# Reading a transposed operand in runs of eight: the column-major half of a four-way scan's input projection

## The chip, the cores and the metric

The kernel runs on one core of a Trainium2 chip. The core has five engines that run side by side, each with a queue of its own that it works through strictly in order: TensorE (PE, matrix products, with weight loads listed apart as PEld), VectorE (DVE), ScalarE (ACT), GpSimd (POOL) and SyncE (SP, which here only starts DMA transfers). Engines wait for one another through semaphores. Operands lie in the on-chip memory (SBUF, 128 partitions). TensorE writes its products into PSUM, and ACT or DVE take them out from there; this is called an eviction. The metric is the device time of one execution in microseconds.

## The reference, cut to what matters

The network takes images x of shape (8, 64, 64, 96): eight images of 64 by 64 points with 96 channels. The part that the change touches is the input of a selective scan in four directions:

```
xz = einsum('bhwc,ec->bhwe', group_norm(x), in_proj_w)      # 96 -> 2 * 192
xin, z = split(xz, 2)
xc = silu(depthwise_conv3x3(xin) + conv_b)                  # b, 192, h, w
x_hw = xc.reshape(b, 192, 4096)                             # row-major
x_wh = transpose(xc, (0, 1, 3, 2)).reshape(b, 192, 4096)    # column-major
xs = stack([x_hw, x_wh, flip(x_hw), flip(x_wh)])            # four directions
x_dbl = einsum('bkdl,kcd->bkcl', xs, x_proj_weight)         # 192 -> 6 + 16 + 16 per direction
dts, Bs, Cs = split(x_dbl, [6, 22])
```

Behind that come the step sizes delta = softplus(dt_proj(dts)), the scan h = h * exp(delta * A) + delta * u * B with y = sum(h * C) over 16 states, the sum of the four directions, a normalization, a gate and an output projection, and then an attention block and a small quantized feed-forward block. Everything is in float32 where the change is made. The flipped directions use the same u and only other weights, so the kernel makes two projections per image: o = 0 over u in row-major order and o = 1 over u in column-major order, each for two directions at once.

## The kernel before, in words

The kernel has three passes, one behind the other. `pass1` (line 233) makes everything that the scans need: group norm, input projection, convolution with SiLU, x_proj, and the splitting of its results into bfloat16 parts. `pass2` (line 513) does the scans, `pass3` (line 819) the rest. The change lies in pass 1 alone.

Channels lie on the partitions. Images are taken in pairs. The 192 channels of a pair fill three chunks of 128 partitions: chunk 0 and chunk 1 are the first 128 channels of the two images, chunk 2 holds the last 64 of both. The order is 0, 2, 1 (`ORDER`, line 248). One chunk of u is a tile of 128 x 4096 (h, w row-major); four of these may be open at a time (`UB`, line 238).

- `projection` (line 348) transposes 512 points of x on TensorE (`pt`), normalizes them on DVE (`xn`), multiplies them by the weights (`pa`) and lets ACT evict them into the padded image `xpad` and the gate `z`. `statistics` (line 305) does the same transposes ahead of that (`xs`, `pt`), and DVE takes the group statistics `st`; `group_norm` finishes them through two tiny products (`pm`, `pv`).
- `convolution` (line 397) makes nine DVE instructions of 128 x 4096 for one chunk, and then on ACT the SiLU: four instructions that read a quarter of the columns of u and write it, turned to column-major, into `ut` (two buffers, each stored to `u_d[b][1]` by SP), then two instructions that put SiLU onto u in place, half by half, and a store of u to `u_d[b][0]`. The bookkeeping marks u as finished (`done["u", ...]`) with the last of these.
- `x_projection` (line 445) takes 512 points of one image and one order: two products that add up in one PSUM bank `px` (three banks), an eviction to `xd` (three buffers) by ACT, or by DVE for every second group of the last pair, and a store to `xd_d`. For o = 1 the product reads u with a step of one image row, 64 float32 values, from each element to the next. Each float32 product appears in the trace as two records.
- `split` (line 469) loads rows of `xd_d` back (`bq`), rounds them on ACT (`bs`), subtracts on POOL (for the last image on DVE) and stores the parts.

The instructions of each engine are issued in an order that is fixed when the program is built. `weave` (line 140) is a small planner: each unit (one call of the functions above) announces its next step with an engine and an assumed cost in microseconds (`yield "act", 2.1`), and the planner always issues the step that could begin first by its own clock. So a changed cost in a `yield` changes the order of instructions on every engine in pass 1. The class `InOrder` (line 81) issues each of them, which is why nearly all rows of the profile carry line 89; its rows are told apart by tile names. Passes 2 and 3 have plans of their own and issue the same instructions in the same order in both kernels.

Of the kernel before, what the change touches and what calls it, by code (L numbers as in the profile page):

```python
# [33 lines left out]
F32 = mybir.dt.float32  # L34
# [3 lines left out]
AF = mybir.ActivationFunctionType  # L38
# [4 lines left out]
P = 128  # L43
NB, HH, WW, C = 8, 64, 64, 96
L = HH * WW
DI, N, R, K = 192, 16, 6, 4
NXD = R + 2 * N
# [11 lines left out]
RPG = GRP // WW  # L59
# [6 lines left out]
def chunk_rows(pair, c):  # L66

    b0 = 2 * pair
    if c < 2:
        return [(slice(0, P), b0 + c, slice(0, P))]  # L70
    return [(slice(64 * j, 64 * j + 64), b0 + j, slice(P, DI)) for j in range(2)]
# [161 lines left out]
def pass1(ctx, tc, g, consts, ident, mhalf, engines, u_d, z_d, xd_d, b_d, dt_d):  # L233
    nc = tc.nc
    pe, dve, act, pool = engines
    sp = InOrder(tc, nc.sync)
# [3 lines left out]
    two = ctx.enter_context(tc.tile_pool(name="p1two", bufs=2))  # L240
# [19 lines left out]
    conv_b = wp.tile([P, 2, 1], F32, name="conv_b")  # L260
# [26 lines left out]
    pts, mms, pxs = Slots(2), Slots(3), Slots(3)  # L287
    counts = {}

    def one_more(key, of, end):  # L290
        counts[key] = counts.get(key, 0) + 1
        if counts[key] == of:
            done[key] = end
# [103 lines left out]
    def convolution(pair, c):  # L397

        ty = c // 2
        src = xpad[c + pair % 2 if c == 2 else c]  # L400
        for b in [2 * pair, 2 * pair + 1] if c == 2 else [2 * pair + c]:
            yield "proj", b
        before = {0: (pair - 1, 1), 2: (pair, 0), 1: (pair, 2)}[c]
        at = 3 * pair + ORDER.index(c) - UB
        if at >= 0:
            old, c_old = at // 3, ORDER[at % 3]
            for b in {0: (2 * old,), 1: (2 * old + 1,), 2: (2 * old, 2 * old + 1)}[c_old]:
                yield "xproj", b
            yield "stored", old, c_old
        if before[0] >= 0:  # L410
            yield "conv", *before
        u = None
        for tap in range(9):
            end = yield "dve", 2.6 if tap == 0 else 4.4, 0.0
            if tap == 0:
                u = us_p.tile([P, L], F32, name="u")
                us[pair, c] = u
                uv = u.rearrange("p (h w) -> p h w", w=WW)
            win = src[:, tap // 3 : tap // 3 + HH, tap % 3 : tap % 3 + WW]
            if tap == 0:  # L420
                dve.tensor_scalar(uv, win, conv_w[:, ty, tap : tap + 1], None, ALU.mult)
            else:
                dve.scalar_tensor_tensor(uv, win, conv_w[:, ty, tap : tap + 1], uv, ALU.mult, ALU.add)
        done["conv", pair, c] = end
        if before[0] >= 0:
            yield "stored", *before
        parts = chunk_rows(pair, c)
        for w in (slice(i, i + WW // 4) for i in range(0, WW, WW // 4)):
            yield "act", 2.1
            ut = two.tile([P, L // 4], F32, name="ut")  # L430
            act.activation(ut.rearrange("p (w h) -> p h w", h=HH), uv[:, :, w], AF.Silu, bias=conv_b[:, ty, :])
            yield "sp", 0.5
            for part, b, ch in parts:
                sp.dma_start(u_d[b][1][ch, w.start * HH : w.stop * HH], ut[part, :])
        for h in range(2):
            cols = slice(h * (L // 2), (h + 1) * (L // 2))
            end = yield "act", 2.0
            act.activation(u[:, cols], u[:, cols], AF.Silu, bias=conv_b[:, ty, :])
        done["u", pair, c] = end
        end = yield "sp", 0.5  # L440
        for part, b, ch in parts:
            sp.dma_start(u_d[b][0][ch, :], u[part, :])
        done["stored", pair, c] = end

    def x_projection(b, o, q):
        pair, j = b // 2, b % 2
        yield "u", pair, j
        yield "u", pair, 2
        px = None
        for ty, u in ((0, us[pair, j]), (1 + j, us[pair, 2])):  # L450
            end = yield ("pe", 0.9, 0.4) if px else ("pe", 0.9, 0.4, pxs)
            if px is None:
                px, slot = ps_px.tile([P, GRP], F32, name="px", tag="px"), pxs.taken
            if o == 0:
                src = u[:, q * GRP : (q + 1) * GRP]
            else:
                src = u.rearrange("p (h w) -> p w h", w=WW)[:, q * RPG : (q + 1) * RPG, :]
            pe.matmul(px, w_xp[:, ty, o, :], src, start=ty == 0, stop=ty > 0)
        one_more(("xproj", b), 2 * NG, end)
        by_dve = pair == NB // 2 - 1 and q % 2 == 1  # L460
        end = yield ("dve" if by_dve else "act"), 0.6
        xd = three.tile([2 * NXD, GRP], F32, name="xd")
        (dve.tensor_copy if by_dve else act.copy)(xd, px[0 : 2 * NXD, :])
        pxs.release(slot, end)
        end = yield "sp", 0.9, 3.0
        sp.dma_start(xd_d[b][o][:, q * GRP : (q + 1) * GRP], xd)
        one_more(("xd", b, o), NG, end)
# [26 lines left out]
    for pair in range(NB // 2):  # L494
        batches = (2 * pair, 2 * pair + 1)
        for b in batches:
            units += [("stats", statistics(b, q)) for q in range(NG)]
            units.append(("norm", group_norm(b)))
            units += [("proj", projection(b, q)) for q in range(NG)]
        for c in ORDER:  # L500
            units.append(("conv", convolution(pair, c)))
        for b in batches:
            for o in range(2):
                units += [("xproj", x_projection(b, o, q)) for q in range(NG)]
                units += [("split", split(b, o, 0, 2 * N, 4, at, b_d[b][o])) for at in (0, GRP)]
                units.append(("split", split(b, o, DT0, 2 * R, 8, 0, dt_d[b][o])))
# [595 lines left out]
```

## Time and profile before

| What | Value |
|---|---|
| Time, median of 8 runs | 10575.13 us (10571.86 to 10589.52) |
| The profiled execution's own time | 10577.66 us |
| Its span, first to last instruction | 10575.9 us |
| Mean granted TensorE clock | 0.899 of full |
| Pass 1, until the first loads of pass 2 can start | about 830 us of the span |
| Busy over the span | DVE 91%, ACT 88%, POOL 88%, PE 73% |

The busy shares of the whole span are those of pass 2, which takes most of it. What the change can move is decided in the first 830 us, and for these the views are asked for single stretches. A "records" count of a tile named px counts two for each product. "A <- B" in a list of waits means that an instruction writing A stood idle until B was done. The chain of waits is followed backwards from the last instruction of a window, so it shows in each stretch what ended last there.

### The profile page before, as it was taken

Reading aid. Unit: us, or ns where it says so; the run is one execution under the profiler, and the core shown is the slowest. Engines: PE = TensorE matmul, PEld = TensorE weight load, DVE = VectorE, ACT = ScalarE, POOL = GpSimd, SP = SyncE. Lnnn points to the kernel's source line nnn. Section 1 sums busy time; section 2 is a strip of 40 time slices with the busy share of each in tenths; the row PEclk is TensorE's granted clock in tenths of the full one; section 3 lists DMA queues with packets and bytes.
Section 4 is the critical chain, followed back from the end, with each engine's and each line's share of the span. In section 5 each row is a group of like instructions: output and inputs, shape, how many; then the busy total and the mean of one; then the engine's idle time right before and its main releaser. Section 6 shows DMA issues by size and latency. Waiting matters only on the chain.

```text
span 10575.9 us, 151369 instructions
## 1 busy us (share of the span) xinstructions
PE 7706.9 (73%) x51232; PEld 6204.6 (59%) x51232; DVE 9635.6 (91%) x6994; ACT 9299.9 (88%) x21355; POOL 9258.9 (88%) x3259
## 2 busy tenths in 40 slices
PE   6876777777677777777677777776777777776887
PEld 3325666566556666666566666665566666555775
DVE  7767999999999999999999999999999999997776
ACT  4648999999999999999999999999999999996665
POOL 2547999999999999999999999999999999997886
PEclk8988999998999999988999999889999999987776
DMA  5756666679986666698966666889766667997442
GB/s 153 218 184 196 209 212 218 209 216 200 197 216 213 212 215 209 213 206 195 211 216 209 217 212 216 206 199 205 216 211 210 219 208 216 201 199 178 127 125 64
DMA packets 928009, 2103.22 MB, mean 199 GB/s; under 512 B 274391, under 2 KB 422648, under 8 KB 925700
## 3 DMA queue, kind: packets, MB, share of 16 engines
q1 hardware_dynamic: 919812, 2092.79, 70.7%
q8 instruction: 410, 6.72, 0.3%
q14 instruction: 363, 2.97, 0.1%
q10 hardware_dynamic: 7424, 0.74, 0.1%
HBM read 1917.59 MB, written 175.66 MB: 198 GB/s over the span
## 4 chain that ended last, share of the span: by engine, by line
ACT 28%; DVE 21%; PE 18%; issue 17%; POOL 13%; DMA 3%; SPq 1%; DVEq 0%; ACTq 0%; POOLq 0%
DVE h L89 15%; ACT x L89 13%; ACT da L89 10%; POOL c L89 9%; PE wide L89 6%; PE acc L89 6%; DVE wide L89 3%; PE px L89 2%; PE mm L89 2%; ACT L89 1%; DMA xdt<-dt_d 1%; PE pa L89 1%; POOL xg L89 1%; DVE u L89 1%; ACT delta L89 1%
## 5 line engine op out<-in xcount | busy, mean ns | idle before, releaser
L89 POOL TENSOR_TENSOR c<-c,h 128x2048 f32<-128x2048 f32 x1536 | 6967.9, 4550 | 398.9 <-DVE h L89 339.5
L89 DVE TENSOR_TENSOR_SCAN h<-da,carry,wide 128x1024 f32<-128x1024 f32 x2304 | 5253.9, 2331 | 204.6 <-PE wide L89 137.8
L89 ACT ACTIVATE x<-duT,bT 128x128 f32<-128x128 f32 (+1 forms) x14336 | 4155.6, 366 | 56.8 <-PE wide L89 50.5
L89 PE MATMUL acc<-ident,c 128*128 128x128 f32 x24576 | 3489.3, 298 | 546.5 <-POOL c L89 538.1
L89 ACT ACTIVATE da<-delta,a_neg 128x1024 f32<-128x1024 f32 x3072 | 3505.1, 1144 | 352.6 <-DVE h L89 341.4
L89 PEld LDWEIGHTS acc<-ident,c 128*128 128x128 f32 x24576 | 3139.9, 155 | 885.5 <-POOL c L89 750.3
L89 PE MATMUL wide<-ident,x 128*128 128x128 f32 x11264 | 1607.8, 291 | 863.4 <-DVE h L89 847.2
L89 PEld LDWEIGHTS wide<-ident,x 128*128 128x128 f32 x11264 | 1338.4, 149 | 1159.1 <-DVE h L89 507.8
L89 DVE TENSOR_TENSOR_SCAN h<-da,wide 128x1024 f32<-128x1024 f32 x768 | 1707.4, 2270 | 89.2 <-PE wide L89 65.8
L89 DVE TENSOR_TENSOR wide<-du,wide 128x1024 f32<-128x1024 f32 x1216 | 1459.1, 1212 | 143.4 <-PE wide L89 143.2
L89 PE MATMUL wide<-xb,sel 96*128 96x512 bf16 x2432 | 753.9, 395 | 587.5 <-DVE h L89 496.6
L89 POOL TENSOR_TENSOR xg<-duT,bT 128x512 f32<-128x512 f32 (+1 forms) x640 | 892.2, 1409 | 79.2 <-PE wide L89 57.8
L89 PEld LDWEIGHTS <-sel 96*128 96x128 bf16 x2432 | 223.6, 101 | 777.2 <-DVE h L89 387.5
L89 PE MATMUL wide<-ident,xg 128*128 128x128 f32 x3584 | 500.3, 285 | 241.3 <-DVE h L89 235.4
L89 PEld LDWEIGHTS wide<-ident,xg 128*128 128x128 f32 x3584 | 412.4, 146 | 317.4 <-issue 154.9
L89 POOL TENSOR_TENSOR du<-delta,u 128x1024 f32<-128x1024 f32 x192 | 455.3, 2371 | 149.3 <-ACT delta L89 139.5
L89 ACT ACT_TABLE_LOAD x385 | 494.0, 1283 | 6.8
L89 DVE SCALAR_TENSOR_TENSOR u<-xpad,conv_w,u 128x4096 f32<-128x4096 f32 x96 | 449.6, 4684 | 1.1
L89 PE MATMUL px<-u,w_xp 128*128 128x512 f32 x512 | 369.7, 871 | 66.3 <-ACT u L89 42.3
L89 PE MATMUL mm<-w_out,gt 128*128 128x96 f32 (+1 forms) x1024 | 260.9, 374 | 37.7 <-POOL gt L89 18.8
L89 POOL TENSOR_TENSOR bq<-bq,bs 128x512 f32<-128x512 f32 (+1 forms) x42 | 135.8, 3244 | 157.3 <-ACT bs L89 157.3
L89 PEld LDWEIGHTS px<-u,w_xp 128*128 128x128 f32 x512 | 106.5, 216 | 273.0 <-issue 173.3
(133 smaller groups left out, 6064.3 us busy)
## 6 DMA issues: line engine op xcount, KB each, us to landing
c<-xd_d SPq DMA_DIRECT2D x1024, 1024.0 KB
c<-xd_d SPq DMA_DIRECT2D x1024, 512.0 KB
u<-u_d SPq DMA_DIRECT2D x128, 512.0 KB
xdt<-dt_d SPq DMA_DIRECT2D x1152, 36.0 KB
xb<-b_d SPq DMA_DIRECT2D x384, 96.0 KB
u<-u_d SPq DMA_DIRECT2D x128, 256.0 KB
y_d<-y SPq DMA_DIRECT2D x24, 1024.0 KB
y<-y_d SPq DMA_DIRECT2D x64, 384.0 KB
```

The costliest lines, as they stand in the source:

```text
L89: ins = getattr(self.engine, op)(*args, **kwargs).ins
```

## The change

Five things change in two functions.

1. The column-major product (o = 1) no longer reads u in column order. It reads the same 8 columns of all 64 rows as they lie: for each row a run of eight neighbouring values. The 512 results stand in `px` in the order (row, column).
2. The eviction of that product turns them: it reads PSUM with a step of eight values and writes `xd` in the column-major order that it had before.
3. In `convolution` the two SiLU instructions in place come first, and u is marked finished with them. The four turning instructions come behind and are plain copies of the finished u (no SiLU, no bias). The stores of `ut` and u follow in the order they had.
4. Every second eviction goes to DVE only for the last image (b = 7), not for both images of the last pair.
5. The planner's assumed costs change: 0.62 for a px product (0.9 before), 0.8 for the turning eviction (0.6 before).

```diff
         parts = chunk_rows(pair, c)
-        for w in (slice(i, i + WW // 4) for i in range(0, WW, WW // 4)):
-            yield "act", 2.1
-            ut = two.tile([P, L // 4], F32, name="ut")
-            act.activation(ut.rearrange("p (w h) -> p h w", h=HH), uv[:, :, w], AF.Silu, bias=conv_b[:, ty, :])
-            yield "sp", 0.5
-            for part, b, ch in parts:
-                sp.dma_start(u_d[b][1][ch, w.start * HH : w.stop * HH], ut[part, :])
         for h in range(2):
             cols = slice(h * (L // 2), (h + 1) * (L // 2))
             end = yield "act", 2.0
             act.activation(u[:, cols], u[:, cols], AF.Silu, bias=conv_b[:, ty, :])
         done["u", pair, c] = end
+        for w in (slice(i, i + WW // 4) for i in range(0, WW, WW // 4)):
+            yield "act", 2.1
+            ut = two.tile([P, L // 4], F32, name="ut")
+            act.copy(ut.rearrange("p (w h) -> p h w", h=HH), uv[:, :, w])
+            yield "sp", 0.5
+            for part, b, ch in parts:
+                sp.dma_start(u_d[b][1][ch, w.start * HH : w.stop * HH], ut[part, :])
         end = yield "sp", 0.5
...
-            end = yield ("pe", 0.9, 0.4) if px else ("pe", 0.9, 0.4, pxs)
+            end = yield ("pe", 0.62, 0.4) if px else ("pe", 0.62, 0.4, pxs)
...
-                src = u.rearrange("p (h w) -> p w h", w=WW)[:, q * RPG : (q + 1) * RPG, :]
+                src = u.rearrange("p (h w) -> p h w", w=WW)[:, :, q * RPG : (q + 1) * RPG]
             pe.matmul(px, w_xp[:, ty, o, :], src, start=ty == 0, stop=ty > 0)
...
-        by_dve = pair == NB // 2 - 1 and q % 2 == 1
-        end = yield ("dve" if by_dve else "act"), 0.6
+        by_dve = b == NB - 1 and q % 2 == 1
+        end = yield ("dve" if by_dve else "act"), 0.6 if o == 0 else 0.8
         xd = three.tile([2 * NXD, GRP], F32, name="xd")
-        (dve.tensor_copy if by_dve else act.copy)(xd, px[0 : 2 * NXD, :])
+        src, dst = px[0 : 2 * NXD, :], xd
+        if o == 1:
+            src, dst = src.rearrange("p (h w) -> p w h", w=RPG), xd.rearrange("p (w h) -> p w h", w=RPG)
+        (dve.tensor_copy if by_dve else act.copy)(dst, src)
```

## The prediction

> **What bounds the kernel now.** I read the page first, then busy time by stretch, the chain of waits, the list of waits and single tiles. The change touches only pass 1, the first 830 us; so every gain or loss must be found there, and the page's shares, which are those of the scans, say little. Busy time by stretch (columns: stretch, its length, then PE, PEld, DVE, ACT, POOL in us with instructions, granted clock, DMA share, GB/s):
>
> ```profile
> core 0: us, PE busy (x) PEld busy (x) DVE busy (x) ACT busy (x) POOL busy (x), PEclk, DMA share, GB/s
> 77.00:204.00 127.00, 79.17 (x265) 41.46 (x264) 122.77 (x71) 62.29 (x78) 17.87 (x4) 0.81 0.64 186
> 204.00:633.00 429.00, 368.29 (x842) 143.93 (x841) 342.03 (x151) 249.11 (x341) 234.57 (x67) 0.92 0.65 201
> 633.00:731.00 98.00, 64.73 (x90) 19.52 (x89) 85.40 (x22) 40.21 (x45) 47.06 (x13) 0.81 0.58 175
> 731.00:830.00 99.00, 65.02 (x87) 18.20 (x85) 15.90 (x25) 31.20 (x41) 13.73 (x12) 0.83 0.55 181
> ```
>
> Up to 204 us the convolution fills DVE. From 204 to 633 PE is the fullest (368 of 429 us) and DVE stands still for 87. From 633 to 731 DVE does two convolutions with little else; after 731 none is left, and PE's projections of the last two images lead to the end of the pass. Two stretches of products alone (same columns without POOL, px instructions only), and pieces of the chain of waits (start, us, what):
>
> ```profile
> 456.50:460.60 4.10, 3.60 (x8) 1.50 (x8) 0.00 (x0) 0.58 (x1) 1.00 0.77 213
> 781.00:808.00 27.00, 27.00 (x32) 6.19 (x30) 2.75 (x4) 2.33 (x4) 1.00 0.34 107
> ```
> ```profile
> 335.17 6.87 PE px L89 x8
> 376.45 10.46 DMA xd_d<-xd
> 457.07 3.44 PE px L89 x8
> 718.29 30.32 PE px L89 x36
> 772.03 36.03 PE px L89 x46
> ```
>
> At a granted clock of 1.00, eight row-major records take 3.44 us (0.43 each), eight column-major ones 6.87 (0.86 each; the 32 of the last image fill 27 us). So a column-major product costs 1.72 us and a row-major one 0.86. At a granted clock of 0.50 (773 to 776.5) row-major records also follow each other at 0.855: there a faster read could gain nothing. Who waited from 204 to 633 on DVE (us, times, longest), and what the ACT and DVE steps take (min/median/max ns):
>
> ```profile
> DVE xn L89 <- PE pt L89: 50.3, 16, 12.5
> DVE st L89 <- PE pt L89: 16.1, 9, 4.1
> DVE gm L89 <- PE pm L89: 8.3, 1, 8.3
> DVE u L89 <- PE px L89: 7.4, 1, 7.4
> ```
> ```profile
> L89 ACT ACTIVATE ut<-u,conv_b x48: 2029/2091/2188, 121.6 to 752.5; 128x1024 f32<-128x1024 f32 x48
> L89 ACT ACTIVATE u<-u,conv_b x24: 1986/2002/2020, 131.5 to 759.1; 128x2048 f32<-128x2048 f32 x24
> ```
> ```profile
> L89 ACT COPY xd<-px x112: 566/582/641, 193.9 to 806.4; 76x512 f32<-76x512 f32 x112
> L89 DVE COPY xd<-px x16: 677/686/689, 703.6 to 808.1; 76x512 f32<-76x512 f32 x16
> ```
>
> 82 of DVE's 87 idle us wait for PE: small transposes and statistics products queue behind px products. Turned writes cost ACT twice the time per element (1024 in 2.09 us against 2048 in 2.00).
>
> **The change part by part.** *The read.* The 128 column-major products are 256 records. Their new price is bounded by 0.43 (all steps contiguous) and 0.86 (all steps 256 B). Seven of eight steps are now contiguous, which is nearest to the row-major row; mixing the two by steps, 7/8 x 0.43 + 1/8 x 0.86, I take 0.48. That frees 0.38 x 32 = 12 us per image. [...]
>
> *From 204 to 633.* The column-major groups of images 0 to 4 lie here (first to last weight load: 215 to 252, 308 to 346, 392 to 424, 483 to 524, 566 to 601), so 5 x 12 = 60 us of PE go. In this stretch the chain of waits names px for 43.5%, pa for 17.4%, pt for 5.7%: PE is what ends last for two thirds. I let two thirds of the 60 arrive: 40. DVE's 82 us of waits for PE leave room for that. What is late next are the loads that transposes wait for (xs 17.8 us, xt 16.4 us already) and stores of xd (three buffers; one piece of 10.46 us above).
>
> *From 633 to 731.* The group of image 5 (639 to 667) gets 12 us shorter under two convolutions: no gain, DVE covers it. The convolution's last chunk loses DVE's five evictions before 731 (5 x 0.69) and the 11.9 us in which DVE stood before one of them at 716: it ends some 15 us earlier. That is not on the path as long as PE still has image 6 to do.
>
> *From 695 to 808.* PE starts image 6 at 695.4, behind ACT's turned writes (689.4 to 693.3) and SiLU. With SiLU first it starts 4 us earlier. Image 6's column-major group fills PE from 722.7 to 750.3, 27.4 us. PE then stands idle until 756.6 for SiLU of the last chunk, whose convolution was over at 731.3 but which sat behind turned writes and evictions in ACT's queue: those 6.3 us go. Image 7's column-major group is 27.4 us too. With a contiguous read matmuls alone would be 15.4 us, but the pure row-major groups show what the three xd buffers allow: 21 us for image 2 (370.3 to 391.5). I take 21 for both: 2 x 6.4. Sum of this stretch: 4 + 6.4 + 6.3 + 6.4 = 23.
>
> *The eviction.* The trace shows no PSUM read with a step. Below: 0.58 on ACT and 0.69 on DVE, since the same elements move and nothing can become shorter. Above: the turned write's factor of 2.09, 1.22 and 1.43. Each element now lies apart, like those of the turned write, so I take the upper end. 60 evictions on ACT cost 60 x 0.64 = 38 us, and the eight moved from DVE 5 to 9 us more; ACT is idle for 180 of 429 us, and a px bank still has 1.9 us of products per eviction. Only the last one, on DVE, lies on the path: 0.7 us. If ACT had no idle time there, the 38 would count.
>
> *The moved copies.* 48 turning instructions keep their 2.09 us as copies (an ACT copy of 512 takes 0.58, a SiLU 0.60), and 64 stores on SP go with them. They now stand behind SiLU and among evictions, on ACT and on SP: an eviction or an xd store behind a copy waits 2.09 us more, covered by two other px banks. The u store stays last, so u buffers come free as before. POOL's splits only move with the xd stores. The assumed 0.62 us for a product that takes 0.96 lets ACT meet evictions early and wait at them, as now (0.9 against 1.72).
>
> *Sum.* 40 + 23 - 1 = 62. The profiled execution took 10577.7 and is 2.5 us above the median of the eight runs: 10577.7 - 62 = 10516, and 10513 against the median.
>
> **The rivals.**
> *Freed PE time runs into loads.* The small transposes wait for xs and xt (34 us), xd stores land late, and after each such idle stretch the clock is granted at 0.50, at which the new read is no faster. Interleaved row-major groups (image 1: 265 to 302, image 3: 445 to 482) span as long as column-major ones (308 to 346, 483 to 524), which speaks for it; PE at 86% against it. Then only about a third of the last stretch and 10 us of the middle remain: 20 us, 10555. [...]
> *The change doesn't speed the read.* If a jump every eight values costs as much as one at each, products stay at 1.72. What remains is 4 + 6 us from SiLU first: 10565. Against it, seven in eight steps are those of the fast row.
> *Slower: copies that wait for their buffer hold ACT.* There are two ut buffers, so the third and fourth copy of a chunk wait for a store to land (before: 16.0 us in 9 waits, longest 4.0). Now evictions queue behind them. Eight chunks release projections, so 16 such waits count, and three px banks cover 3 x 1.72 = 5.2 us. At 9 us per wait the 62 us are gone (16 x 3.8); at 10.5, like the longest xd landing, the loss is 85 and the result 23 slower: 10598. Against it: the 4.0, and evictions stand between the copies in the new order on ACT, so stores have time.
> *More than forecast.* All of the 60 in the middle, the last groups at 15.4 and the clock high: 60 + 10 + 19 + 6 = 95, and up to the 14 us per image: 10465.
>
> **How the numbers follow.** A measurement of this kernel tells about 0.2%, 21 us. Forecast (30 to 110 us gained) 0.66, more than that 0.05, loads 0.12 (half of it beyond 21 us), read not faster 0.06, slower 0.11 (nearly all of it beyond 21 us). So faster 0.79 (0.66 + 0.05 + 0.06, and 0.02 of the unfast read), same 0.11, slower 0.10. Range: below 10465 lies the 0.05; above 10568 lie the slower case and a part of the unfast read, 0.14. The eviction's and the read's bounds move the sum by less than that.
>
> **What would show it.** Right: column-major px records at 0.43 to 0.50 where the clock is 1.00; px busy down from 370 to about 280 us; DVE's waits for PE in the middle halved; xd evictions on ACT with a second length of up to 1.2 us; px of the last image beginning within 12 us of the last convolution; the first loads of pass 2 some 60 us earlier and passes 2 and 3 as long as before. Wrong: records still at 0.86; ACT or SP idle before evictions for a ut store; PE idle before transposes for xs and xt by as much as px lost.

## The result and the profile after

The changed kernel takes 10541.18 us (median of 10 runs, 10530.59 to 10552.66) against 10576.31 us for the kernel before (28 runs). The ratio is 0.9968, with a 95% interval of 0.9960 to 0.9976: 35 us faster, between 25 and 42. The prediction was 10513, a gain of 62, in a range of 10465 to 10568. So the direction and the range held, and the expected gain is about half there.

Busy time by stretch for the changed kernel (stretch, its length, then PE, PEld, DVE, ACT, POOL in us with instructions, granted clock, DMA share, GB/s). The borders are the start of the third convolution, the start of the last but one, the end of the last one, and the first loads of pass 2:

```profile
core 0: us, PE busy (x) PEld busy (x) DVE busy (x) ACT busy (x) POOL busy (x), PEclk, DMA share, GB/s
173.00:614.00 441.00, 343.92 (x918) 158.09 (x917) 371.48 (x164) 261.21 (x357) 214.58 (x67) 0.88 0.70 214
614.00:703.00 89.00, 42.25 (x78) 15.78 (x76) 88.12 (x18) 41.73 (x48) 69.36 (x15) 0.74 0.63 183
703.00:795.00 92.00, 31.55 (x64) 12.74 (x64) 13.40 (x20) 31.12 (x41) 13.68 (x12) 0.70 0.64 199
```

The products themselves and their evictions, from the same kernel's groups of instructions in pass 1 (busy us, mean ns of one | idle before them and what ended it):

```profile
L89 PE MATMUL px<-u,w_xp 128*128 128x512 f32 x512 | 258.3, 643 | 103.0 <-ACT u L89 62.2 <-ACT xd L89 37.4 <-DVE xd L89 3.3
L89 ACT COPY ut<-u 128x1024 f32<-128x1024 f32 x48 | 95.5, 1997 | 7.6 <-DMA u_d<-ut 7.3
L89 ACT COPY xd<-px 76x512 f32<-76x512 f32 x120 | 69.6, 585 | 169.1 <-DMA xd_d<-xd 136.8 <-PE px L89 25.3 <-DMA u_d<-ut 3.8
L89 DVE COPY xd<-px 76x512 f32<-76x512 f32 x8 | 5.5, 687 | 55.5 <-DMA xd_d<-xd 47.2 <-DMA b_d<-bs 5.8 <-DMA u_d<-ut 2.4
```

The same groups in the kernel before:

```profile
L89 PE MATMUL px<-u,w_xp 128*128 128x512 f32 x512 | 369.7, 871 | 66.3 <-ACT u L89 42.3 <-ACT xd L89 22.1 <-DVE xd L89 1.9
L89 ACT COPY xd<-px 76x512 f32<-76x512 f32 x112 | 65.0, 583 | 194.9 <-PE px L89 119.9 <-DMA xd_d<-xd 44.9 <-issue 25.6
L89 DVE COPY xd<-px 76x512 f32<-76x512 f32 x16 | 11.0, 685 | 78.2 <-PE px L89 52.0 <-DMA xd_d<-xd 14.4 <-issue 11.9
```

PE's time on x_proj products fell from 369.7 to 258.3 us, by 111. The turning eviction costs nothing: half of the evictions after the change turn, and the mean is 585 ns on ACT where it was 583, 687 on DVE where it was 685. What grew is ACT's wait for xd stores, from 44.9 us to 136.8.

Where the 111 us went is read from events that occur in both kernels:

| Event | before | after | gained so far |
|---|---|---|---|
| chunk 2 of the last pair, convolution starts | 633.3 | 614.1 | 19 |
| last convolution ends | 731.3 | 702.8 | 28 |
| first product of image 7 | 756.6 | 723.6 | 33 |
| last eviction ends | 808.8 | 763.8 | 45 |
| first xb load of pass 2 is issued | 829.1 | 794.9 | 34 |
| first scan starts | 856.5 | 819.6 | 37 |

Second profiles of both programs put the first scan at 855.1 and 822.3, and the start of chunk 2 at 630.9 and 613.1; so pass 1 repeated within 3 us in these two programs. In a third one that was profiled twice (the old costs, below) it moved by 7. Passes 2 and 3 vary more: from the first scan on they took 9719.4 and 9704.2 us in the two profiles of the kernel before, 9710.5 and 9710.4 in those of the changed one, and 9698.2 to 9722.9 over all kernels below. That is why the first scan, and not the span, is compared below wherever a part of pass 1 is meant.

### The profile page after: what moved, and what is told of

Its sections match the earlier page's. It is cut to its first block, busy times and chain, and to the rows that moved or that the text cites. A ratio compares the mean times of both kernels' runs of the same rounds, so it can differ in the third digit from the quotient of the medians.

```text
span 10530.1 us, 151336 instructions
## 1 busy us (share of the span) xinstructions
PE 7600.9 (72%) x51232; PEld 6187.7 (59%) x51232; DVE 9638.4 (92%) x6986; ACT 9295.1 (88%) x21363; POOL 9251.6 (88%) x3259
## 4 chain that ended last, share of the span: by engine, by line
ACT 28%; DVE 20%; issue 17%; PE 14%; POOL 11%; DMA 3%; SPq 1%; DVEq 0%; POOLq 0%; ACTq 0%
DVE h L89 15%; ACT x L89 13%; ACT da L89 10%; POOL c L89 8%; PE wide L89 6%; PE acc L89 5%; DVE wide L89 4%; PE mm L89 2%; ACT L89 1%; POOL xg L89 1%; ACT delta L89 1%; ACT y L89 1%; ACT duT L89 1%; SPq L89 1%; DMA xdt<-dt_d 1%
## 5 line engine op out<-in xcount | busy, mean ns | idle before, releaser
L89 PE MATMUL px<-u,w_xp 128*128 128x512 f32 x512 | 258.3, 643 | 103.0 <-ACT u L89 62.2
L89 PEld LDWEIGHTS mm<-w_out,gt 128*128 128x128 f32 (+1 forms) x1024 | 199.2, 240 | 101.4 <-issue 31.8
L89 PE MATMUL wide<-ident,du 128*128 128x128 f32 x1536 | 210.4, 282 | 62.3 <-DVE h L89 44.5
```

The costliest lines, as they stand in the source:

```text
L89: ins = getattr(self.engine, op)(*args, **kwargs).ins
```

## The experiments

Two theories stood first. *Read*: the gain comes from the faster column-major read, and what is missing was lost in waits for xd buffers. *Order*: the gain is u being finished earlier. A third, *plan*, puts it on the planner's new costs. The read and the order of SiLU were each done alone, the order and the costs each undone alone; DVE's shorter list was not run by itself.

**The read alone.** The kernel before with

```diff
-                src = u.rearrange("p (h w) -> p w h", w=WW)[:, q * RPG : (q + 1) * RPG, :]
+                src = u.rearrange("p (h w) -> p h w", w=WW)[:, :, q * RPG : (q + 1) * RPG]
...
-        (dve.tensor_copy if by_dve else act.copy)(xd, px[0 : 2 * NXD, :])
+        src, dst = px[0 : 2 * NXD, :], xd
+        if o == 1:
+            src, dst = src.rearrange("p (h w) -> p w h", w=RPG), xd.rearrange("p (w h) -> p w h", w=RPG)
+        (dve.tensor_copy if by_dve else act.copy)(dst, src)
```

> The kernel before with the read in runs of eight and the turning eviction alone; order of SiLU, assumed costs and DVE's share of evictions as before. Theory 'read': px busy falls from 370 to about 260 us, yet the time falls by only 15 to 30 us, and ACT's wait for xd stores grows from 45 us towards 100. Theory 'order': at most 10 us faster. Theory 'plan' (the new assumed costs and the shorter DVE list make the gain): at most 10 us faster too.

Measured: 10518.79 us, ratio 0.9949 (0.9936 to 0.9963), 54 us faster: more than the whole change. px busy is 266.6 us, ACT's wait for xd stores 83.2. All three theories missed the size. Chunk 2 of the last pair starts at 590.9, 42 us earlier than before, and the first scan at 807.4, 49 earlier. So the changed kernel holds something that loses part of what the read alone gives.

**SiLU first alone.** The kernel before with the two in-place SiLU instructions first and the four turning copies behind.

> The kernel before with SiLU first and plain turning copies behind alone; column-major read as before. Theory 'read': 0 to 12 us faster, px busy stays near 370 us. Theory 'order': 20 to 35 us faster, as the whole change.

Measured: 10553.77 us, ratio 0.9978 (0.9969 to 0.9988), 19.5 us faster, px busy 363.3. That lies between the theories. But its profile shows the first scan at 853.6, only 3 us earlier, and chunk 2 of the last pair starts 12 us *later* (645.6). The last SiLU starts earlier (751.7, before 759.1) even though the last convolution ends later (749.3, before 731.3): the new order helps at the end of the pass and hurts in the middle. Where the other 16 us of the measured gain lie isn't settled; in the profile they are in passes 2 and 3, whose instructions are the same and whose time varies by that much from one execution to another.

**SiLU first undone.** The changed kernel with the old order of SiLU and turned writes.

> The changed kernel with one part undone: the turned SiLU writes come first again, as in the kernel before, and u is finished behind them. Theory 'read' (the gain comes from the faster column-major read, and most of what that read freed is lost again in waits for the three xd buffers): still 15 to 30 us faster than before, px busy stays near 258 us. Theory 'order' (most of the gain is u being finished earlier): at most 10 us faster than before.

Measured: 10535.96 us, ratio 0.9964 (0.9951 to 0.9976), 37 us faster, as the changed kernel. *Order* falls: on top of the read the new order adds nothing to the time, though the first scan comes at 826.5 without it, 4 to 7 us later than in the changed kernel. *Read* had 15 to 30 and missed too, on the other side. This kernel differs from the one with the read alone by the assumed costs and by DVE's shorter list of evictions, and it is 17 us slower than that one.

**Old costs.** The changed kernel with 0.9 us assumed for a product and 0.6 for each eviction.

```diff
-            end = yield ("pe", 0.62, 0.4) if px else ("pe", 0.62, 0.4, pxs)
+            end = yield ("pe", 0.9, 0.4) if px else ("pe", 0.9, 0.4, pxs)
...
-        end = yield ("dve" if by_dve else "act"), 0.6 if o == 0 else 0.8
+        end = yield ("dve" if by_dve else "act"), 0.6
```

> The changed kernel with the planner's old assumed costs (0.9 for a product, 0.6 for each eviction). Theory 'read': within 10 us of the changed kernel, that is 25 to 45 us faster than before. Theory 'plan': at least 15 us of the gain are gone.

Measured: 10520.51 us, ratio 0.9952 (0.9939 to 0.9964), 53 us faster. *Plan* falls with the wrong sign: undoing the costs doesn't lose 15 us, it gains some. *Read*, with at most 45, missed as well. Since both profiles had the first scan at the same place, this was measured again beside the changed kernel:

> The changed kernel once more, beside the next kernel on one chip. Both theories: 25 to 45 us faster than before. Its profile shows how much pass 1 and passes 2 and 3 vary from one execution of the same program to another: if the first scan starts within 3 us of 819.6, pass 1 repeats, and what differs between executions lies behind it.

> The changed kernel with the planner's old assumed costs once more. Theory 'costs lose' (the new assumed costs give back 15 to 20 us of the gain): 10 us or more faster than the changed kernel beside it. Theory 'no difference' (the two profiles show first scans at 819.6 and 820.6 us, so pass 1 is equally long): within 8 us of it.

Measured: 10535.12 us (0.9967, 0.9954 to 0.9979) and 10522.39 us (0.9956, 0.9944 to 0.9969). Both lie within what was expected of them, the second as theory *costs lose* had it: the old costs are 13 us faster than the new ones here and 21 in the first comparison; with SiLU last the step is 17 (the two kernels above, DVE's list included). The sign is the same three times, while the intervals still overlap, so some 15 us is a likely price and not a sharp one. Where it lies depends on the order of SiLU. With SiLU first the profiles place little of it in pass 1; with SiLU last they place 19 us there (826.5 against 807.4). All four plans with the fast read, with two values where a program was profiled twice:

| Plan, with the fast read | chunk 2 of the last pair starts | DVE's waits for PE from 200 us to there | first scan | faster than before |
|---|---|---|---|---|
| SiLU last, old costs (the read alone) | 590.9 | 39 | 807.4 | 54 |
| SiLU first, old costs | 618.5, 612.2 | 65, 61 | 820.6, 813.8 | 53, 50 |
| SiLU last, new costs | 622.4 | 70 | 826.5 | 37 |
| SiLU first, new costs (the change) | 614.1, 613.1 | 55, 60 | 819.6, 822.3 | 35, 37 |

The last three have DVE's shorter list too; set beside SiLU first alone (old costs too, long list), the traces of the old costs show the same order of instructions on every engine up to 672 us, so the list doesn't touch the second and third columns. Up to there either departure from the old plan takes 21 to 32 us of the 42 that the read gives, and both together take no more: undoing one of them alone brings nothing back. In the time of the whole kernel only the costs tell.

> The kernel before once more, for its profile alone: the first scan within 3 us of 856.5 us if pass 1 repeats from execution to execution; passes 2 and 3 may differ by some 10 us, as the profiles of the other kernels do (9701 to 9723 us), though their instructions are the same.

Measured: the first scan at 855.1, and 9704.2 us from there to the end, 15 less than in the other profile of the same program. It took 10561.05 us in all.

**Where the middle is lost.** In the changed kernel, the timeline of 196 to 220 us shows one loss whole. DVE, then ACT (start, us, instruction, idle time before it and what ended that), then PE's waits in the stretch 173 to 233:

```profile
201.35 0.69 DVE L89 BATCH_NORM_STATS2 st<-pt 96x6 f32<-96x512 f32 x1 [4.19 <-PE pt L89]
...
219.52 0.69 DVE L89 BATCH_NORM_STATS2 st<-pt 96x6 f32<-96x512 f32 x1 [8.09 <-PE pt L89]
```
```profile
205.56 0.58 ACT L89 COPY xd<-px 76x512 f32<-76x512 f32 x1 [0.94 <-PE px L89]
215.92 0.58 ACT L89 COPY xd<-px 76x512 f32<-76x512 f32 x1 [9.78 <-DMA xd_d<-xd]
```
```profile
PE px L89 <- ACT xd L89: 13.0, 6, 7.5
```

SP issued the store of u (two transfers of 1024 KB) at 199.4, right behind the last turned quarters. The xd stores issued after it let ACT wait 9.8 us for a free xd buffer; the px banks stayed full, PE stood up to 7.5 us before the next product; the small transposes behind that product in PE's queue came late, and DVE, which has the convolution to do, stood 8.1 us before a statistics step. The convolution of chunk 1 of the first pair thus takes from 172.7 to 232 us, against 172 to 219 before. Earlier products meet the stores of the same chunk's u; later ones (before the change) came when those stores were on their way. That the store of u is what delays them is read from the order of issue; no run shows it by itself. How long DVE waits for PE from about 200 us to the start of the last pair's chunk 2 was 82 us before and 90 with SiLU first alone; the table above has the kernels with the fast read, where the read alone stands out with 39 (it issues all instructions in the order of the kernel before). This loss belongs to SiLU first: with SiLU last and the new costs the fourth convolution starts at 222.6, and that kernel loses its time later. The waits of DVE with the read alone:

```profile
DVE xn L89 <- PE pt L89: 19.5, 7, 5.2
DVE st L89 <- PE pt L89: 14.5, 8, 4.5
```

**The xd buffers.** Theory *ring*: three buffers are what holds back the freed time. Theory *traffic*: xd stores are late because of the 2 MB stores of u ahead of them, and more buffers only move the wait. Room for five came from making the constant `sel2` behind pass 1.

```diff
+    xd_p = ctx.enter_context(tc.tile_pool(name="p1xd", bufs=5))
...
-        xd = three.tile([2 * NXD, GRP], F32, name="xd")
+        xd = xd_p.tile([2 * NXD, GRP], F32, name="xd")
```

> The changed kernel with five xd buffers in place of three (room comes from making the constant sel2, 4 KB per partition, behind pass 1 instead of ahead of it). Theory 'ring' (what the faster read freed is lost at the three xd buffers): ACT's wait for xd stores falls from 137 us to under 70, and the kernel is 55 to 80 us faster than before, against 35 for the changed kernel. Theory 'traffic' (xd stores land late because 2 MB stores of u are ahead of them, and more buffers only move the wait): within 10 us of the changed kernel, 25 to 45 us faster than before.

> The kernel before with five xd buffers (sel2 made behind pass 1). Theory 'ring': products at 1.72 us each are the slower step there, so 0 to 15 us faster than before. Theory 'traffic': within 10 us of before.

> The changed kernel with two xd buffers in place of three. Theory 'ring': the gain is gone; between 5 us faster and 40 us slower than before, with ACT's wait for xd stores over 200 us. Theory 'traffic': at least 20 us faster than before.

Measured: 10513.46 us with five buffers in the changed kernel (0.9950, 0.9936 to 0.9963: 60 us faster than before); 10550.45 with five in the kernel before (0.9981, 0.9972 to 0.9989: 23 faster); 10575.26 with two in the changed kernel (1.0005, 0.9996 to 1.0014: no gain left). ACT's wait for xd stores in these three, in that order:

```profile
ACT xd L89 <- DMA xd_d<-xd: 71.5, 25, 14.3
```
```profile
ACT xd L89 <- DMA xd_d<-xd: 16.0, 8, 4.6
```
```profile
ACT xd L89 <- DMA xd_d<-xd: 193.4, 69, 12.5
```

*Traffic* missed all three. *Ring* had the times of the changed kernel, 25 us from two more buffers and 35 lost with one less (its bounds for the waits, under 70 and over 200, were just missed), but not that of the kernel before, where it gave 0 to 15 and 23 came. The buffers are thus not the place where the freed time in particular was lost: two more of them are worth 23 to 25 us with either read, though the wait there was 45 us in one kernel and 137 in the other. Some 14 us of each gain are in pass 1 (first scan at 805.3 and 841.6). The runs with five also make `sel2` behind pass 1, which was not run alone; DVE spends 1.3 us on it.

The loss at 220 us is still there with five buffers. DVE, and PE's longest wait in the stretch 173 to 233:

```profile
222.52 0.69 DVE L89 BATCH_NORM_STATS2 st<-pt 96x6 f32<-96x512 f32 x1 [12.47 <-PE pt L89]
```
```profile
PE pt L89 <- DMA xs<-in_x: 16.3, 5, 14.2
```

PE no longer stands for an xd buffer there (1.4 us in all), but the transposes that come next wait 14.2 us for their load of x (`xs`): SP issued it at 202.8, behind the store of u at 198.7. With SiLU first and the old costs it is the same (8.0 and 7.5 us in the two profiles, and DVE stands 9.0 and 9.3). So an xd buffer is only one of two ways in which this place loses time; in both, a transfer issued right behind the store of u comes late.

**The store of u in pieces.** The changed kernel with eight pieces that the planner sets 4.5 us apart:

```diff
-        end = yield "sp", 0.5
-        for part, b, ch in parts:
-            sp.dma_start(u_d[b][0][ch, :], u[part, :])
+        for i in range(0, L, L // 8):
+            end = yield "sp", 0.5, 4.0
+            for part, b, ch in parts:
+                sp.dma_start(u_d[b][0][ch, i : i + L // 8], u[part, i : i + L // 8])
```

> The changed kernel with the 2 MB store of u in eight pieces that the planner sets 4.5 us apart. Theory 'traffic': xd stores pass between the pieces, ACT's wait for them falls by half, 50 to 75 us faster than before. Theory 'ring': within 10 us of the changed kernel, 25 to 45 us faster than before.

Measured: 10603.5 us, ratio 1.0029 (1.0017 to 1.0040), 30 us slower than before. Both theories missed. The run doesn't test *traffic*: the planner lets a chunk's SiLU begin only when the chunk before it is fully stored, so the pieces held back the next chunk. From the fourth convolution's start to the fifth's 104 us pass (233 to 337; 232 to 281 in the changed kernel), and up to chunk 2 of the last pair PE waits 60 us for SiLU before products. Whether smaller stores would help if SiLU didn't wait for them stays open.

**Read and buffers together.** The read alone (old order, old costs, old DVE list) with five xd buffers:

> The kernel before with the read in runs of eight and the turning eviction alone (old order of SiLU, old costs), and five xd buffers. If the read's gain (54 us in the run with it alone) and the buffers' (23 us on the kernel before) add up: 70 to 85 us faster than before, the fastest of all. If both cure the same wait: 50 to 65 us.

Measured: 10500.02 us, ratio 0.9937 (0.9924 to 0.9949): 72 us faster than before and the fastest of all, twice the gain of the change. The two gains, 54 and 23, add up but for 5, so they don't cure the same wait. The first scan starts at 799.9; ACT's wait for xd stores is

```profile
ACT xd L89 <- DMA xd_d<-xd: 27.4, 15, 4.9
```

## Why the prediction was right, and by how much it missed

*The bound and the place.* Right. Everything is found in pass 1; the first scan moved by 37 us in the first pair of profiles, by 33 in the second, and the median by 35.

*The read.* Right, on the fast side. The bounds were 0.43 and 0.86 us per record, 0.48 was taken. The last ten records of image 7, column-major ones, fill 4.56 us where eight row-major ones had filled 3.60, both at a granted clock of 1.00: 0.46 and 0.45 each, with the end of the last one counted; from start to start it is 0.43, the row-major price. The median of all 512 px records fell from 1034 to 592 ns. px busy fell by 111 us where 96 were forecast (8 x 12): 13.9 us per image. *More than forecast* counted with 14; that is the lower bound of 0.43 on 32 records, which no run had shown for a read in runs of eight before the result.

*From 204 to 633: 40 us.* For the read this was right: done alone it gains 42 up to the start of that chunk. For the change it was wrong: 19. One step that failed is "the moved copies", which was said to cost an eviction or an xd store 2.09 us at most, "covered by two other px banks". SiLU first alone starts that chunk 12 us later than before. The delay is not the copy's length: earlier products put their evictions and xd stores into the time in which ut and u are stored, and there one xd store holds ACT for 9.8 us, more than the banks cover; with five buffers a load behind the same store of u holds PE for 14.2.

*Assumed costs at nothing.* This too failed. "As now" was the argument; the runs make the new costs some 15 us slower in three comparisons, and with SiLU last they alone move the start of that chunk (one profile each) from 590.9 to 622.4. So the 19 can't be put down to the copies alone: either step would have brought the 40 down to about that. What PE and the plan say fits it, without showing it: a product now takes 0.86 us, which the old 0.9 met and the new 0.62 doesn't.

*From 633 to 731.* DVE's last two convolutions were forecast 15 us shorter, and off the path. They took 9 less (98.0 to 88.7; four evictions, not five, stood ahead of the end), and the last convolution's end did come onto the path.

*From 695 to 808: 23 us.* From the start of that chunk on, the last eviction came another 26 us earlier. The size fits, the terms don't, and that their sum holds is luck. SiLU first, image 6's shorter products and the 6.3 us (16.7 together) ended in one wait: PE was through with image 6 at 702.8 and stood 20.8 us for the SiLU of the last chunk, where it had stood 6.3. In front of that SiLU, ACT stood for an xd store that was issued behind the store of u at 689.9:

```profile
710.12 0.58 ACT L89 COPY xd<-px 76x512 f32<-76x512 f32 x1 [11.18 <-DMA xd_d<-xd]
```

In their place came the 9 us of the last convolution, 4 or 5 by which SiLU and image 7 followed its end sooner (20.8 us behind it; the prediction had at most 12 as a sign of being right), and 12 from image 7, where 6.4 was forecast. Not in the sum was a step behind it: from the last eviction to the first xb load of pass 2 it was 20 us and is now 31. In the chain of waits of the changed kernel the end of the pass reads (start, us, what)

```profile
702.71 11.65 DMA xd_d<-xd
715.37 5.03 DMA bq<-xd_d
723.59 5.50 PE px L89 x6
...
755.98 6.99 DMA u_d<-ut
774.68 5.14 DMA bq<-xd_d
786.26 7.61 DMA xdt<-dt_d
```

The last turned quarter is now stored after most evictions, at 756, and u behind it, ahead of the last loads of `bq`; the prediction wrote that the u store "stays last, so u buffers come free as before" and did not ask what it stands in front of. The splits of `bq` crowd there too. PE is no longer in this chain but for 5.5 us.

*The eviction.* The upper end, 1.22 us, was taken and the lower was true: 0.585 on ACT. It cost nothing in the sum, since it was counted as covered.

*The rivals.* Freed PE time running into xd stores and loads is what happened in the middle, though not for want of buffers alone; PE's waits for xs and xt did not grow in total (from 200 us to that chunk 17 us after, 40 before). The slower case named ACT's queue behind turned writes; the holder of that queue was the xd buffer, with up to 11.2 us at once, and the ut buffer only 7.3 us in all.

## What to carry to other kernels

Undo each part of a change by itself before calling the whole a gain: here one part alone gave 54 us, and the parts beside it took 19 away. When something becomes ready earlier, ask which transfers are in flight at that time and what waits in order behind the first step that meets them. Undoing one part alone can also mislead: in the middle either of two parts was enough to lose half of the gain, and only the run with neither showed it. A growing wait in the profile is not a price: two more buffers were worth 23 us where ACT's wait was 45, and 25 where it was 137.

## What the runs showed of the hardware

An ACT or DVE read of PSUM with a step of eight float32 values cost no more here than a contiguous one (means of 585, with half of the evictions turning, against 583 ns for 76 x 512 on ACT; 687 against 685 on DVE). ACT's turned copy, which reads runs of 16 values and writes SBUF with a step of 64, took twice the time per element of the contiguous SiLU (1024 in 1997 ns, 2048 in 2002). At a granted clock of 1.00 a float32 product that reads runs of eight values, 256 B apart, ran at the rate of a contiguous one (ten records in 4.56 us, where eight contiguous ones took 3.60), one that jumps at each value at half of it (0.86 us per record against 0.43). At a granted clock of 0.50 the contiguous one took 0.855 (773 to 776.5 us in the kernel before). The same program's passes 2 and 3 took 9719 and 9704 us in two executions; the cause wasn't looked for.
